# A graph-attention layer on one core: one-hots change engines, messages read their weights from PSUM, gathered rows enter as transposes

## The chip, the core and the metric

The kernel runs on one core of a Trainium2 chip. The core has TensorE (PE; PEld is its load of the stationary operand), VectorE (DVE), ScalarE (ACT), GpSimd (POOL) and SyncE (SP), which take their instructions in order and meet through semaphores. The two on-chip memories are SBUF and PSUM; PE writes its products into PSUM[...], and DVE and ACT can read and write PSUM too. The metric is device time in microseconds (us), the median of several runs.

## The reference, cut to what matters

A graph of 12500 nodes (128 features) and 200000 edges, sorted by destination, goes through two layers. The first is an attention layer with 4 heads of 32 channels:

```
xl, xr = x @ W_l, x @ W_r
e     = einsum(leaky_relu(xl[src] + xr[dst], 0.2), att)     # per edge and head
p     = exp(e - segment_max(e, dst)[dst])
out   = segment_sum(p / segment_sum(p, dst)[dst] * xl[src], dst) + bias + x
x1    = layernorm(x + layernorm(out) * gamma + beta)
```

with a self loop added for every node. The second layer takes `segment_sum(x1[src] + edge_attr, dst)`, a small two-matrix network and another layer norm.

## The kernel before

**Three stages.** A first stage (to about 60 us) computes xl for all nodes and stores it in DRAM as `xl_d`. The first layer (to about 2150 us) and the second (to the end) then go through the edges in 112 chunks of 1792: 128 partitions x T = 14 edges each. Because the edges are sorted, the destinations of a chunk span at most 128 consecutive nodes.

**The gathers.** For every chunk, `gather` (L186) issues 14 indirect DMAs on POOL, each of 128 rows of 512 bytes, into a tile `got` with four buffers. The first layer gathers from `xl_d`, the second from `x1_d`. The indices `srcs` lie in SBUF.

**One chunk of the first layer.** The functions below are called once per chunk c, several of them per quarter q (`quads`: three of 4 and one of 2 of the 14 columns).

- `nodes1/2/3` and `parts2/3` (L244 to L279) compute the destination side: xr of the chunk's nodes, split into three bf16 parts whose sum is the f32 value.
- `node_by_edge` (L281) builds a bf16 one-hot `odt`, nodes by edges, from the loaded destination numbers `row`, with one DVE compare per quarter (L285).
- `products` (L289) sums in PSUM tile `ph` (three buffers) xr[dst] and xl[src], transposed: three bf16 products of the parts with `odt` (L294), then for each column the gathered rows times an identity (L297).
- `leaky` (L300): ACT writes 0.2 times `ph` to `lk` (L304), DVE takes the larger of the two (L305).
- `away` (L309) and `edge_by_node0` (L315) build the other one-hot `od`, edges by nodes, in f32 on ACT: 14 times Abs(iota - rel), then one Relu(1 - od) over all columns (L312, L317).
- `scores` (L319): PE multiplies `lk` with the attention vector (L325).
- `weights1` to `weights5` (L332 to L385): running maxima of the scores over the edges of a node, by scans (L329) within a partition and across partitions, with transposes on PE between; then `val` gets the exponentials (L382).
- `messages` (L387): DVE multiplies the gathered rows with the exponentials, both in SBUF (L390).
- `sums` (L394): 14 products of `od` with `val` into `ps` (L398).
- `merge1`, `merge2`, `carry` (L402 to L433) bring in the self loop and a node that is cut by a chunk's end; `norm1a`, `roots`, `norm1b`, `norm2` (L458 to L487) do the layer norms of two chunks together and store x1.

**Order.** The loop at L499 writes out the order by hand: each engine's queue holds the instructions in the order of the calls. Iteration c works on chunk c (products to scores), on chunk c - 1 (weights to sums), on c - 2 (merge) and c - 3 (carry, norms), and prepares the destination side of c + 1. The gathers of c + 1 and, on SP, the loads of `row` and `x` for c + 2 are issued at its start. Tiles have two buffers unless noted.

The second layer's `edge_by_node` (L192) keeps its Abs and Relu on ACT.

Of the kernel before, what the change touches and what calls it, by code (L numbers as in the profile page):

```python
# [8 lines left out]
F32 = mybir.dt.float32  # L9
BF16 = mybir.dt.bfloat16  # L10
I32 = mybir.dt.int32
AF = mybir.ActivationFunctionType
OP = mybir.AluOpType
# [3 lines left out]
P = 128  # L17
D = 128
H = 4
C = D // H  # L20
HW = C + 1
AW = H * HW
RW = AW + H
VW = RW + 1
T = 14
CE = P * T
# [119 lines left out]
def fast_path(ctx: ExitStack, tc: tile.TileContext, a: dict, out: bass.AP, g: dict):  # L146
    nc = tc.nc
# [67 lines left out]
    with tc.tile_pool(name="ew", bufs=2) as ew, \  # L215
# [3 lines left out]
        keep = []  # L219
        for i in range(2):  # L220
            mask = ew.tile([P, H * S + 1], F32, name=f"mask{i}", bufs=1)
            nc.vector.memset(mask[:, H * S:], LOW)
            rf = ew.tile([H, P + 1], F32, name=f"rf{i}", bufs=1)
            nc.vector.memset(rf[:, 0:1], LOW)
            rb = ew.tile([H, P + 1], F32, name=f"rb{i}", bufs=1)
            nc.vector.memset(rb[:, P:], LOW)
            keep.append((mask, rf, rb))
        live = {}

        def put(name, c, tile_):  # L230
            live[name, c] = tile_
            return tile_
# [32 lines left out]

        def parts2(c):
            parts = live["parts", c]
            r1 = put("r1", c, ew.tile([P, D], F32, name="r1"))
            nc.vector.tensor_sub(r1, live.pop(("pn", c))[:, 3, :], parts[:, 0, :])
            nc.scalar.copy(parts[:, 1, :], r1)  # L270

        def parts3(c):
            parts = live["parts", c]
            nc.vector.tensor_sub(parts[:, 2, :], live.pop(("r1", c)), parts[:, 1, :])

        def nodes3(c):
            pm = ep.tile([P, 4 * P], F32, name="pm", bufs=2)
            nc.tensor.matmul(pm[:, :H], live.pop(("lks", c)), attm, start=True, stop=True)
            nc.vector.tensor_copy(live["sr", c][:, AW:RW], pm[:, :H])  # L279

        def node_by_edge(c, q):  # L281
            if q == 0:
                put("odt", c, ew.tile([P, CE], BF16, name="odt"))
            t0, m = quads[q]
            nc.vector.tensor_scalar(live["odt", c][:, t0 * P:(t0 + m) * P],  # L285
                                    live["row", c][:, t0 * P:(t0 + m) * P], nid[:, c:c + 1], None,
                                    op0=OP.is_equal)

        def products(c, q):  # L289
            t0, m = quads[q]  # L290
            ph = put("ph", (c, q), ep.tile([P, 4 * P], F32, name="ph", bufs=3))
            parts, odt, got = live["parts", c], live["odt", c], live["got", c]
            for k in range(3):
                nc.tensor.matmul(ph[:, :m * P], parts[:, k, :], odt[:, t0 * P:(t0 + m) * P],  # L294
                                 start=(k == 0), stop=False)
            for t in range(m):
                nc.tensor.matmul(ph[:, t * P:(t + 1) * P], got[:, t0 + t, :], ident,  # L297
                                 start=False, stop=(t == m - 1))

        def leaky(c, q):  # L300
            t0, m = quads[q]
# [2 lines left out]
            nc.scalar.mul(lk[:, :m * P], ph[:, :m * P], 0.2)  # L304
            nc.vector.tensor_max(lk[:, :m * P], ph[:, :m * P], lk[:, :m * P])  # L305


        def away(c, t0, t1):
            if t0 == 0:  # L309
                put("od", c, ew.tile([P, T, P], F32, name="od"))  # L310
            for t in range(t0, t1):
                nc.scalar.activation(live["od", c][:, t, :], iota[:, 0, :], AF.Abs,  # L312
                                     bias=nrel[:, c, t:t + 1])

        def edge_by_node0(c):  # L315
            od = live["od", c]
            nc.scalar.activation(od, od, AF.Relu, bias=1.0, scale=-1.0)  # L317

        def scores(c, q):  # L319
            t0, m = quads[q]  # L320
# [8 lines left out]
            nc.vector.tensor_tensor_scan(o, m, d, LOW, op0=OP.add, op1=OP.max)  # L329


        def weights1(c):  # L332
            mask, rf, rb = keep[c % 2]
            s = put("s", c, ew.tile([P, H * S], F32, name="s"))
            sv = s.rearrange("p (h s) -> p h s", h=H)
            nc.vector.memset(sv[:, :, 0:S:S - 1], LOW)
            nc.vector.tensor_scalar(mask[:, :H * S].rearrange("p (h s) -> p h s", h=H),
                                    same[:, c, None, :].to_broadcast([P, H, S]), -1.0, -LOW,
                                    op0=OP.add, op1=OP.mult)
            nc.scalar.copy(sv[:, :, 1:T + 1], live.pop(("sc", c)))  # L340
            fwd = put("fwd", c, ew.tile([P, H * S], F32, name="fwd"))
            bwd = put("bwd", c, ew.tile([P, H * S], F32, name="bwd"))
            scan(fwd, mask[:, :H * S], s)
            scan(bwd[:, ::-1], mask[:, :0:-1], s[:, ::-1])
# [24 lines left out]
        def weights5(c):  # L369
            mask, rf, rb = keep[c % 2]  # L370
            pm, s, fwd, bwd = (live.pop((k, c)) for k in ("pm", "s", "fwd", "bwd"))
            sv = s.rearrange("p (h s) -> p h s", h=H)
            nc.vector.tensor_copy(sv[:, :, 0:S:S - 1],
                                  pm[:, :2 * H].rearrange("p (k h) -> p h k", h=H))
            scan(fwd, mask[:, :H * S], s)
            scan(bwd[:, ::-1], mask[:, :0:-1], fwd[:, ::-1])
            mv = bwd.rearrange("p (h s) -> p h s", h=H)[:, :, 1:T + 1]
            arg = ew.tile([P, H, T], F32, name="arg")
            nc.vector.tensor_sub(arg, sv[:, :, 1:T + 1], mv)
            v = put("val", c, ew.tile([P, T, VW], F32, name="val"))  # L380
            vh = v[:, :, :AW].rearrange("p t (h c) -> p t h c", h=H)
            nc.scalar.activation(vh[:, :, :, C], arg.rearrange("p h t -> p t h"), AF.Exp)  # L382
            nc.scalar.copy(v[:, :, RW], lastf[:, c, :])
            nc.vector.tensor_mul(v[:, :, AW:RW], mv.rearrange("p h t -> p t h"),
                                 lastf[:, c, :, None].to_broadcast([P, T, H]))  # L385

        def messages(c, q):  # L387
            t0, m = quads[q]
            vh = live["val", c][:, t0:t0 + m, :AW].rearrange("p t (h c) -> p t h c", h=H)
            nc.vector.tensor_mul(vh[:, :, :, :C],  # L390
                                 live["got", c][:, t0:t0 + m, :].rearrange("p t (h c) -> p t h c", h=H),
                                 vh[:, :, :, C:].to_broadcast([P, m, H, C]))

        def sums(c):  # L394
            ps = put("ps", c, ep.tile([P, VW], F32, name="ps"))
# [98 lines left out]
        parts2(0)  # L494
        parts3(0)
        nodes3(0)
        for q in range(4):
            node_by_edge(0, q)
        for c in range(NCH + 2):  # L499
            on, nxt, prv, old = c < NCH, c + 1 < NCH, 0 < c <= NCH, c > 1  # L500
            k = (c - 3) // 2
            if c + 2 < NCH:
                load0(c + 2)
            if nxt:
                put("got", c + 1, gather(ew, xl_d, c + 1))
            if on:
                products(c, 0)
            if prv:
                weights1(c - 1)
            if on:  # L510
                away(c, 0, 3)
                leaky(c, 0)
            if prv:
                weights2(c - 1)
            if c > 2:
                carry(c - 3)
            if on:
                away(c, 3, 5)
                products(c, 1)
            if prv:  # L520
                weights3(c - 1)
            if on:
                leaky(c, 1)
                scores(c, 0)
            if old:
                merge1(c - 2)
            if prv:
                weights4(c - 1)
            if nxt:
                nodes1(c + 1)  # L530
            if prv:
                weights5(c - 1)
            if old:
                merge2(c - 2)
            if on:
                products(c, 2)
                leaky(c, 2)
                away(c, 5, 8)
                scores(c, 1)
            if nxt:  # L540
                nodes2(c + 1)
            if prv:
                messages(c - 1, 0)
            if nxt:
                parts2(c + 1)
            if prv:
                messages(c - 1, 1)
            if nxt:
                parts3(c + 1)
            if on:  # L550
                products(c, 3)
                leaky(c, 3)
                scores(c, 2)
            if prv:
                messages(c - 1, 2)
                messages(c - 1, 3)
            if nxt:
                nodes3(c + 1)
            if on:
                away(c, 8, T)  # L560
                scores(c, 3)
            if prv:
                sums(c - 1)
            if on:
                edge_by_node0(c)
            if nxt:
                for q in range(4):
                    node_by_edge(c + 1, q)
            if c % 2 == 1 and k >= 0:
                norm1a(k)  # L570
                roots(k)
            if c % 2 == 0 and k >= 0:
                norm1b(k)
                if k > 0:
                    norm2(k - 1)
# [558 lines left out]
```

## Time and profile before

| | |
|---|---|
| median of 3 runs | 4132.05 us (4130.75 to 4137.15) |
| the profiled execution | 4133.73 us, its span 4131.9 us |
| PE busy | 3270.6 us (79%) |
| PEld | 2777.0 us (67%) |
| DVE | 1741.6 us (42%) |
| ACT | 2047.6 us (50%) |
| POOL | 3060.0 us (74%) |
| gathers of the first layer | first 64.2 us, last 2112.7 us |
| gathers of the second layer | first 2150.1 us, last 4113.7 us |

A line of groups reads: source line, engine, operation, output <- inputs, partitions x elements and type, count | busy us in all, mean ns of one | idle time of the engine just before them, and what ended it. A line of the timeline reads: start us, duration us, engine, line, operation, operands, how many in a row, and in brackets the idle time before it and its releaser. "issue" is a wait for nothing that the profile shows. The granted clock is the share of TensorE's full clock that it was allowed.

### The profile page before, as it was taken

What the parts mean: (1) busy time and instruction counts of PE and PEld (TensorE: products, weight loads), DVE (VectorE), ACT (ScalarE), POOL (GpSimd) and SP (SyncE); (2) the same over time, 40 slices, a digit from 0 to 9 for tenths busy, and PEclk for the clock granted to TensorE, in tenths of its full rate; (3) what the DMA queues carried; (4) which work ended last, traced back from release to release, by engine and by line L of the source; (5) the groups of instructions that cost most, each with busy time, mean ns of one, the idle gap of its engine ahead of it and who ended that gap; (6) DMA issues with size and microseconds to landing.
All of it is one profiled execution on the core that took longest, in us unless ns stands there. A gap on an engine that the chain in (4) does not pass through costs nothing. (4 is left out here: it accounts for less than half of the span.)

```text
span 4131.9 us, 59032 instructions
## 1 busy us (share of the span) xinstructions
PE 3270.6 (79%) x19842; PEld 2777.0 (67%) x19842; DVE 1741.6 (42%) x6068; ACT 2047.6 (50%) x5502; POOL 3060.0 (74%) x3141
## 2 busy tenths in 40 slices
PE   5999898998999889989966776776766776766766
PEld 5887777787888778877755555555555555555555
DVE  3777777777777777777750101101010101010101
ACT  2666666666666666566653343434333333333332
POOL 2777777777777777777747777777777777777776
PEclk8989989889888998899887777777777777777776
DMA  6333333333333333333323333333333333333332
GB/s 204 106 107 112 110 105 112 102 112 113 109 107 104 109 112 112 102 113 103 111 72 109 100 120 100 121 100 119 101 111 109 111 109 112 109 103 116 94 118 70
DMA packets 236149, 451.41 MB, mean 109 GB/s; under 512 B 66104, under 2 KB 124601, under 8 KB 235836
## 3 DMA queue, kind: packets, MB, share of 16 engines
q0 software_dynamic: 100384, 205.04, 19.3%
q1 hardware_dynamic: 134876, 240.68, 17.3%
q8 instruction: 157, 2.57, 0.3%
q10 hardware_dynamic: 576, 1.84, 0.1%
q14 instruction: 156, 1.28, 0.1%
HBM read 426.22 MB, written 21.10 MB: 108 GB/s over the span
## 5 line engine op out<-in xcount | busy, mean ns | idle before, releaser
L186 POOL DMA_INDIRECT got<-xl_d,srcs x1568 | 1571.8, 1002 | 541.4 <-issue 505.4
L186 POOL DMA_INDIRECT got<-x_d,srcs x1568 | 1487.0, 948 | 514.0 <-issue 464.1
L613 PE MATMUL ps<-got,od 128*128 128x128 f32 x3136 | 850.6, 362 | 448.1 <-DMA got<-x_d,srcs 443.8
L613 PEld LDWEIGHTS ps<-got,od 128*128 128x128 f32 x3136 | 625.1, 248 | 591.1 <-DMA got<-x_d,srcs 588.6
L612 PE MATMUL ps<-ea,od 128*128 128x128 f32 x3136 | 773.4, 337 | 18.7 <-DMA ea<-in_edge_attr 18.7
L618 DVE SCALAR_TENSOR_TENSOR h<-x1w,ps 128x128 f32<-128x128 f32 x112 | 32.3, 288 | 1556.7 <-PE ps L613 1556.7
L612 PEld LDWEIGHTS ps<-ea,od 128*128 128x128 f32 x3136 | 631.8, 250 | 42.7 <-issue 42.7
L312 ACT ACTIVATE od<-iota,nrel 128x128 f32<-128x128 f32 x1568 | 503.6, 390 | 121.6 <-PE ps L398 121.5
L297 PEld LDWEIGHTS ph<-ident,got 128*128 128x128 f32 x3136 | 445.3, 201 | 164.7 <-DMA got<-xl_d,srcs 112.3
L297 PE MATMUL ph<-ident,got 128*128 128x128 f32 x3136 | 478.2, 290 | 91.1 <-DMA got<-xl_d,srcs 90.8
L398 PE MATMUL ps<-val,od 128*128 128x137 f32 x3136 | 498.7, 328 | 3.6 <-DVE val L390 3.6
L623 ACT COPY ns<-ps 128x128 f32<-128x128 f32 x111 | 29.4, 265 | 948.3 <-DVE h L618 948.3
L325 PE MATMUL sc<-attm,lk 128*128 128x4 f32 x3136 | 427.4, 257 | 71.8 <-DVE lk L305 71.3
L398 PEld LDWEIGHTS ps<-val,od 128*128 128x128 f32 x3136 | 479.8, 234 | 3.7 <-issue 3.7
L198 ACT ACTIVATE od<-iota,nrel 128x128 f32<-128x128 f32 x1568 | 479.9, 387 | 0.0
L325 PEld LDWEIGHTS sc<-attm,lk 128*128 128x128 f32 x3136 | 425.4, 209 | 80.8 <-DVE lk L305 79.5
L305 DVE TENSOR_TENSOR lk<-ph,lk 128x512 f32<-128x512 f32 x448 | 277.9, 620 | 314.4 <-ACT lk L304 314.3
L304 ACT ACTIVATE lk<-ph 128x512 f32<-128x512 f32 x448 | 241.7, 540 | 242.3 <-PE ph L297 242.0
L294 PE MATMUL ph<-odt,parts 128*128 128x512 bf16 (+1 forms) x1344 | 341.5, 365 | 1.3 <-DVE odt L285 1.3
L390 DVE TENSOR_TENSOR val<-got,val 128x512 f32<-128x512 f32 x448 | 267.3, 618 | 0.6 <-issue 0.4
L199 ACT ACTIVATE od<-od 128x896 f32<-128x896 f32 x224 | 212.7, 949 | 7.1
L294 PEld LDWEIGHTS <-parts 128*128 128x128 bf16 x1344 | 133.5, 106 | 96.9 <-issue 35.3
(139 smaller groups left out, 3213.4 us busy)
## 6 DMA issues: line engine op xcount, KB each, us to landing
ea<-in_edge_attr SPq DMA_DIRECT2D x111, 896.0 KB
row<-in_dst_rows SPq DMA_DIRECT2D x336, 256.0 KB
got<-xl_d,srcs POOLq DMA_INDIRECT x1568
got<-x_d,srcs POOLq DMA_INDIRECT x1568
row<-in_dst_rows SPq DMA_DIRECT2D x112, 128.0 KB
xg<-in_x_pad SPq DMA_DIRECT2D x112, 64.0 KB
x_d<-x1w SPq DMA_DIRECT2D x112, 64.0 KB
out<-y SPq DMA_DIRECT2D x111, 64.0 KB
```

The lines of the kernel that those rows point to most:

```text
L186: nc.gpsimd.indirect_dma_start(out=got[:n, t, :], out_offset=None, in_=table[:N, :], in_offset=bass.IndirectOffsetOnAxis(ap=srcs[:n, c, t: ...
L198: nc.scalar.activation(od[:, t, :], iota[:, 0, :], AF.Abs, bias=nrel[:, c, t:t + 1])
L294: nc.tensor.matmul(ph[:, :m * P], parts[:, k, :], odt[:, t0 * P:(t0 + m) * P], start=(k == 0), stop=False)
L297: nc.tensor.matmul(ph[:, t * P:(t + 1) * P], got[:, t0 + t, :], ident, start=False, stop=(t == m - 1))
L304: nc.scalar.mul(lk[:, :m * P], ph[:, :m * P], 0.2)
L305: nc.vector.tensor_max(lk[:, :m * P], ph[:, :m * P], lk[:, :m * P])
L312: nc.scalar.activation(live["od", c][:, t, :], iota[:, 0, :], AF.Abs, bias=nrel[:, c, t:t + 1])
L325: nc.tensor.matmul(live["sc", c][:, :, t0 + t], lk[:, t * P:(t + 1) * P], attm, start=True, stop=True)
L390: nc.vector.tensor_mul(vh[:, :, :, :C], live["got", c][:, t0:t0 + m, :].rearrange("p t (h c) -> p t h c", h=H), vh[:, :, :, C:].to_broadca ...
L398: nc.tensor.matmul(ps, od[:, t, :], v[:, t, :], start=(t == 0), stop=(t == T - 1))
L612: nc.tensor.matmul(ps, od[:, t, :], ea[:, t, :], start=(t == 0), stop=False)
L613: nc.tensor.matmul(ps, od[:, t, :], got[:, t, :], start=False, stop=(t == T - 1))
```

## The change

Only the first layer changes.

- A new PSUM tile `bank` takes one bank: it holds a copy of iota and, behind it, the exponentials of a chunk (`wts`). To make room, `ph` goes from three buffers to two.
- `node_by_edge` moves from DVE to ACT: Abs(row - nid), then Relu(1 - .) in place, over columns 0 to 1023 (half 0) and 1024 to 1791 (half 1).
- The other one-hot, `od`, moves from ACT to DVE: one compare per quarter of iota (from `bank`) with `rel`. It is built one iteration later than before, and has one buffer.
- `weights1` is split: `weights0` prepares its inputs; both now end the iteration of the chunk's own products. `weights5` is split too: `weights6` lets ACT write the exponentials to `wts` and copy them to `val`.
- `messages` reads the exponentials from `wts` in PSUM instead of from `val`.
- `products` first puts the gathered rows into `ph` as PE transposes and then adds the three bf16 products.
- `parts2` keeps its difference in the PSUM tile `pn` instead of an SBUF tile.
- The order of the calls in the loop is new.

```diff
+        bank = ep.tile([P, P + T * H], F32, name="bank")
+        nc.vector.tensor_copy(bank[:, :P], iota[:, 0, :])
+        wts = bank[:, P:].rearrange("p (t h) -> p t h", h=H)
+        nnid = ew.tile([P, NCH], F32, name="nnid", bufs=1)
+        nc.vector.tensor_scalar(nnid, nid, -1.0, None, op0=OP.mult)
...
-        def node_by_edge(c, q):
...
-            nc.vector.tensor_scalar(live["odt", c][:, t0 * P:(t0 + m) * P],
-                                    live["row", c][:, t0 * P:(t0 + m) * P], nid[:, c:c + 1], None,
-                                    op0=OP.is_equal)
+        def node_by_edge(c, i, step):
...
+            lo, hi = (0, 8 * P) if i == 0 else (8 * P, CE)
+            o = live["odt", c][:, lo:hi]
+            if step == 0:
+                nc.scalar.activation(o, live["row", c][:, lo:hi], AF.Abs, bias=nnid[:, c:c + 1])
+            else:
+                nc.scalar.activation(o, o, AF.Relu, bias=1.0, scale=-1.0)
 
         def products(c, q):
...
-            ph = put("ph", (c, q), ep.tile([P, 4 * P], F32, name="ph", bufs=3))
+            ph = put("ph", (c, q), ep.tile([P, 4 * P], F32, name="ph", bufs=2))
             parts, odt, got = live["parts", c], live["odt", c], live["got", c]
+            for t in range(m):
+                nc.tensor.matmul(ph[:, t * P:(t + 1) * P], got[:, t0 + t, :], ident,
+                                 start=(t == 0), stop=False, is_transpose=True)
             for k in range(3):
                 nc.tensor.matmul(ph[:, :m * P], parts[:, k, :], odt[:, t0 * P:(t0 + m) * P],
-                                 start=(k == 0), stop=False)
-            for t in range(m):
-                nc.tensor.matmul(ph[:, t * P:(t + 1) * P], got[:, t0 + t, :], ident,
-                                 start=False, stop=(t == m - 1))
+                                 start=False, stop=(k == 2))
...
-        def away(c, t0, t1):
...
-        def edge_by_node0(c):
-            od = live["od", c]
-            nc.scalar.activation(od, od, AF.Relu, bias=1.0, scale=-1.0)
+        def edge_by_node0(c, q):
+            t0, m = quads[q]
+            if q == 0:
+                put("od", c, ew.tile([P, T, P], F32, name="od", bufs=1))
+            nc.vector.tensor_tensor(live["od", c][:, t0:t0 + m, :],
+                                    bank[:, None, :P].to_broadcast([P, m, P]),
+                                    rel[:, c, t0:t0 + m, None].to_broadcast([P, m, P]), op=OP.is_equal)
...
+        def weights6(c):
+            v = live["val", c]
             vh = v[:, :, :AW].rearrange("p t (h c) -> p t h c", h=H)
-            nc.scalar.activation(vh[:, :, :, C], arg.rearrange("p h t -> p t h"), AF.Exp)
+            nc.scalar.activation(wts, live.pop(("arg", c)).rearrange("p h t -> p t h"), AF.Exp)
+            nc.scalar.copy(vh[:, :, :, C], wts)
             nc.scalar.copy(v[:, :, RW], lastf[:, c, :])
...
         def messages(c, q):
...
-                                 vh[:, :, :, C:].to_broadcast([P, m, H, C]))
+                                 wts[:, t0:t0 + m, :, None].to_broadcast([P, m, H, C]))
```

The calls of an iteration in their new order, with on, nxt, prv, old standing for chunks c, c + 1, c - 1, c - 2 (loads and gathers first, as before; carry of c - 3):

```
prv weights2   prv edge_by_node0(0)   carry   on products(0)
prv weights3   prv edge_by_node0(1)   on leaky(0)   on products(1)   nxt node_by_edge(0, Abs)
prv edge_by_node0(2)   prv weights4   on leaky(1)   prv edge_by_node0(3)   on scores(0)
on products(2)   on leaky(2)   old merge1   nxt nodes1   on scores(1)   on products(3)
prv weights5   on leaky(3)   prv weights6   old merge2   nxt node_by_edge(0, Relu)   on scores(2)
prv messages(0)   nxt nodes2   prv messages(1)   nxt parts2   prv messages(2)   nxt parts3   prv messages(3)
on scores(3)   nxt nodes3   on weights0   on weights1   prv sums
nxt node_by_edge(1, Abs)   nxt node_by_edge(1, Relu)   norms as before
```

## The prediction

> **What bounds the kernel now.** I first read the page's busy shares. PE leads with 79%, but these are means over two layers, so I went to the stretches: in 1000 to 2000 us (first layer) PE is busy 902 us at a granted clock of 0.90, DVE 734, ACT 625, POOL 767; in 3000 to 4000 (second layer) PE is busy 697 and POOL 757. The page's chain of work that ended last covers only the last microsecond and says nothing. The costliest groups say what POOL does, first layer, then second:
>
> ```profile
> L186 POOL DMA_INDIRECT got<-xl_d,srcs x1568 | 1571.8, 1002 | 541.4 <-issue 505.4
> L186 POOL DMA_INDIRECT got<-x_d,srcs x1568 | 1487.0, 948 | 514.0 <-issue 464.1
> ```
>
> The same 1568 gathers last 1002 ns in the first layer and 948 in the second. Between two there is a gap of 0.30 us. 14 gathers x (1.002 + 0.304) = 18.28 us; a chunk takes 18.3 us by the spacing of its repeating rows. So POOL never stops, and its sum is the layer's time: 112 x 18.3 = 2050 us. The waits of 500 to 1500 us (us in all, times, longest) agree:
>
> ```profile
> POOL got L186 <- issue: 211.8, 695, 0.3
> DVE lk L305 <- ACT lk L304: 148.3, 117, 3.6
> PE ph L297 <- DMA got<-xl_d,srcs: 47.5, 44, 2.3
> ```
>
> POOL's waits are the bare gap, whatever name they carry; PE on its part catches up with the gathers and waits for them about 0.9 us a chunk. POOL leads, the others follow.
>
> Next: why 1002 and not 944, the median of both layers? The timeline of POOL, and that of DVE, over one chunk (start us, duration us):
>
> ```profile
> 1037.02 1.44 POOL L186 DMA_INDIRECT got<-xl_d,srcs  x1 [0.30 <-issue]
> 1038.77 1.33 POOL L186 DMA_INDIRECT got<-xl_d,srcs  x1 [0.30 <-issue]
> 1040.40 1.05 POOL L186 DMA_INDIRECT got<-xl_d,srcs  x1 [0.30 <-issue]
> 1041.76 0.94 POOL L186 DMA_INDIRECT got<-xl_d,srcs  x1 [0.30 <-issue]
> ```
>
> ```profile
> 1036.96 0.68 DVE L390 TENSOR_TENSOR val<-got,val 128x512 f32<-128x512 f32 x1
> 1038.10 1.02 DVE L390 TENSOR_TENSOR val<-got,val 128x512 f32<-128x512 f32 x2
> 1039.10 1.53 DVE L285 TENSOR_SCALAR odt<-row,nid 128x512 bf16<-128x512 int32 x4
> 1041.41 0.42 DVE L479 TENSOR_TENSOR x1w<-x1w,L_gnn_ln_gamma 128x256 f32<-128x256 f32 x1
> 1044.49 0.66 DVE L305 TENSOR_TENSOR lk<-ph,lk 128x512 f32<-128x512 f32 x1
> ```
>
> Three of 14 gathers are long: each starts while L390 or L285 runs and is late by about what is left of it (1037.64 - 1037.02 = 0.6 us against 0.5 lost). I laid all POOL rows of 150 to 2050 us over the DVE rows. The 1453 gathers exceed 0.944 us by 83.3 us in all. 168 that overlap an L285 carry 48.1 us of it, 225 more that overlap only an L390 30.0, the rest 5.2. Of 374 that overlap L305 (one input in PSUM) and neither of the two, 5 are over 0.99 us, mean 0.943; 353 beside scans: mean 0.942. Scaled to the layer: 1568 x (1.002 - 0.944) = 91 us lost.
>
> **The change, part by part.**
>
> *L285 goes to ACT, L390 reads its weights from PSUM.* Both long kinds with all inputs in SBUF vanish; L390 becomes L305's kind. A gather then falls to 0.944 + 5.2/1453 + 0.001 = about 0.949, which is also what the second layer shows (0.948). POOL's sum loses 1568 x (1.002 - 0.949) = **83 us**. [...] Such instructions stay: scans 1.17 us a chunk, the small merges 2.2, norms 1.7, about 5.1 us beside 4.3 removed (L390 2.47, L285 1.82). By time held, 4.3/9.4 of 91 us would go: 42 us, 4090. The rows say that the short ones cost 5.2 of 83. I take the row, since a short instruction leaves little to wait for, and keep 42 as an end.
>
> *New one-hots on DVE* (three of 512, one of 256 columns, iota in PSUM): not in the trace; nearest is L305, 0.687 and 0.418 us, so +2.48 us a chunk. L285 (3 x 0.492 + 0.346 = 1.82) goes: DVE +0.66. From below they could go at L285's pace (+0), from above at twice L305's (+3.1). DVE is busy 13.4 us a chunk, and some 45 instructions have 0.03 us between dependent neighbours: 13.4 + 0.7 + 1.3 = 15.4 us dense. [...] L305 from PSUM (687 ns) and L390 from SBUF (684) show none. I add none.
>
> *ACT.* Off: 14 Abs at 1.85/6 = 0.31 and the 1792-wide Relu, 1.70: -6.0. On: Abs and Relu over 1024 and 768 columns; from 1792 in 1.697 and 896 in 0.949 follow 1.06 and 0.84, 3.8 in all, and a small copy 0.2. ACT 11.4 -> 9.4 us a chunk. An int32 input isn't in the trace; at double price ACT has 13.2, still under the gathers.
>
> *Transposes in place of identity products.* L297: 8 records (4 products) in 1.05 us, 0.26 each. The first stage's transposes (L129) take 0.93 us for 7, 0.13 each: PE loses 14 x 0.13 = 1.8 us a chunk, 16.5 -> 14.7. If they cost as much as products, PE stays at 16.5, under 17.5.
>
> All this is hidden: the gathers take 14 x (0.949 + 0.304) = **17.54 us** a chunk, and DVE 15.4, PE 14.7, ACT 9.4 lie beside them. If that cover goes, each 0.1 us a chunk costs 11 us.
>
> *Order and buffers.* No DMA is added or moved; the row loads on SP now wait for ACT's one-hot instead of DVE's, a chunk before use. The gathers on POOL wait only for messages three chunks back. The new ring to watch is ph with two buffers: leaky(0) on DVE, then scores(0) and products(2) on PE, the 0.2 multiple on ACT, then leaky(2) on DVE, with merge1, weights5 and the messages queued behind it. Scores 0.95 (8 records of L325), products 0.5 + 0.65, ACT 0.6, handovers 0.3: 3.0 us, of which one-hots and leaky(1) fill about 2. Bubble 1.0. In every second chunk the root's table loads (1.28 us each) hold the copy of rm: 0.4 on the mean. Followers: 15.4 + 1.0 + 0.4 = 16.8, under 17.54 by 0.7. od with one buffer: the first one-hot waits for the sums of a chunk before, matmul by matmul; from there through the messages to the next sums is about 13.6 us, no bound.
>
> Start and drain: 37 us pass between the layers' gathers (2112.7 to 2150.1). The one-hots add 2.2 us there, scans ahead of the roots save about 1.3: +1, within -3 to +4.
>
> **Sum.** Span 4131.9 and 1.8 around it are 4133.7 for the profiled execution; the median of runs is 1.7 lower. 4133.7 - 83 + 1 - 1.7 = **4050 us**.
>
> **Rivals.**
>
> *A. POOL stays the bound, at clean pace* (above): 4050; with the ends of residue (all 91 us gone, or 25 left) and drain 4038 to 4072. Chance 0.62.
>
> *B. The followers take over part.* The 0.7 us margin is an estimate from rows of another order. At 17.9 us a chunk, 0.4 x 112 = 45 of 91 saved, about 4092; span 4072 to 4123. For it: DVE's waits on ACT's multiple, 2.7 us a chunk now. Against: most of these come where PE waits for gathers. Chance 0.17.
>
> *C. Only the one-hots' share goes* [...]: 48.1/83.3 x 91 = 53 saved, 4080. Against: L305 writes as much. Or nothing goes, because late gathers have another cause: no change, 4132; the overlap counts speak against that. Chances 0.08 and 0.03.
>
> *D. Slower: PE's clock.* [...] The row: the stage before the layers (0 to 60 us), where one PE record in three is a transpose, was granted 0.94, the first layer 0.90, and the second, without transposes in its stream, 0.74. If PE ran at half clock throughout, eight score records take 1.7 us (as they do at 1015.7) and the ring is 5 us long, bubble 3: 15.4 + 3.0 + 0.4 = 18.8 us a chunk, + 0.5 x 112 = 56, 4188. It decides from a bubble of 2.5 on, three quarters of the time at half clock. By today's clock a fifth of it is. Chance 0.10.
>
> **How the numbers follow.** The forecast is A's. The range 4038 to 4095 holds A, C and half of B, about 0.8. Faster by over 0.2% (8 us, about what a measurement of this kernel can tell): A, B and C, 0.87; same 0.03; slower 0.10.
>
> **What would show it.** Right: gathers of got<-xl_d near 0.95 us, none over 1.2 beside the messages; POOL's idle still 0.30 us each; PE's and DVE's waits on got growing or steady. Wrong: POOL waiting for messages by more than the gap (B, D), mean gathers at 0.97 and above (C), clock under 0.7 in the first layer (D).

## The result, and the profile after

The median of six runs after is 4069.28 us (4065.99 to 4072.12), before 4133.47 (six runs): the ratio is 0.9843, with a 95% interval of 0.983 to 0.9856. The change saves 64 us where 82 were forecast; 4069 lies inside the range of 4038 to 4095, 19 us above the 4050 named. The profiled execution took 4072.12 us, its span 4070.3.

The costliest groups of the changed kernel, gathers of the first and second layer (busy us, mean ns, then the idle time before them):

```profile
L186 POOL DMA_INDIRECT got<-xl_d,srcs x1568 | 1501.9, 958 | 540.9 <-issue 488.4 <-PE ph L302 11.9 <-DVE xb L468 4.9
L186 POOL DMA_INDIRECT got<-x_d,srcs x1568 | 1488.5, 949 | 521.1 <-issue 468.0 <-ACT od L198 43.7 <-DMA got<-x_d,srcs 7.9
```

The mean gather of the first layer fell from 1002 to 958 ns, not to the 949 of the prediction. The waits of 500 to 1500 us (total, times, longest) and the busy sums of 1000 to 2000 us (PE, PEld, DVE, ACT, POOL, granted clock, DMA share, GB/s):

```profile
POOL got L186 <- issue: 215.1, 706, 0.3
ACT lk L312 <- PE ph L305: 173.4, 123, 3.9
DVE lk L313 <- ACT lk L312: 106.9, 163, 3.5
```

```profile
1000.00:2000.00 1000.00, 897.64 (x5567) 753.17 (x5622) 800.47 (x2699) 536.22 (x1194) 758.63 (x793) 0.85 0.39 112
```

POOL's waits are still the bare gap of 0.3 us, none longer. So the gathers still set the layer's pace: 14 x (0.958 + 0.304) = 17.67 us against a measured spacing of 17.68 from chunk to chunk (18.30 before). The followers do wait for one another (ACT for the products up to 3.9 us), yet POOL never waits for them. 44 ns on each of 1568 gathers is 70 us, more than the 64 that were saved.

The other term is the drain. POOL stood idle for 43.7 us between the last gather of the first layer (start 2042.2) and the first of the second (2086.9); before it was 36.5: +7 us. -70 + 7 = -63, and the second layer ends 1.6 us later; the span is down by 61.6.

Which gathers are still late? POOL's and DVE's timelines after, over the end of one chunk (start us, duration us):

```profile
1081.13 0.95 POOL L186 DMA_INDIRECT got<-xl_d,srcs  x1 [0.30 <-issue]
1082.38 0.94 POOL L186 DMA_INDIRECT got<-xl_d,srcs  x1 [0.30 <-DVE val L403]
1083.63 1.57 POOL L186 DMA_INDIRECT got<-xl_d,srcs  x1 [0.30 <-issue]
1085.50 0.94 POOL L186 DMA_INDIRECT got<-xl_d,srcs  x1 [0.31 <-issue]
```

```profile
1081.17 0.68 DVE L403 TENSOR_TENSOR val<-got,bank 128x512 f32<-128x512 f32 x1
...
1083.63 0.41 DVE L468 TENSOR_TENSOR xb<-xg,L_gnn_ln_beta 128x256 f32<-128x256 f32 x1
1083.96 0.42 DVE L492 TENSOR_TENSOR x1w<-x1w,L_gnn_ln_gamma 128x256 f32<-128x256 f32 x1
1084.41 0.42 DVE L493 TENSOR_TENSOR x1w<-x1w,xb 128x256 f32<-128x256 f32 x1
```

The gather at 1081.13 begins beside a message (L403) and takes 0.95. The one at 1083.63 begins with the norm's sum of x and beta (L468, two inputs in SBUF), stays behind it and the multiplication by gamma (L492), and takes 1.57.

I sorted all 1568 gathers of each trace by the DVE operation that was in progress 0.1 to 0.2 us after the gather began (a gather can stand in two rows; late is over 0.99 us; the excess is over 0.944):

| DVE operation beside the start | inputs | before: gathers, mean us, late, excess us | after |
|---|---|---|---|
| messages, L390 / L403 | before SBUF + SBUF, after SBUF + PSUM | 236, 1.172, 149, 53.8 | 249, 0.947, 6, 0.8 |
| compare of int32, L285 | SBUF | 118, 1.194, 113, 29.5 | gone |
| one-hots `od`, L319 | PSUM + SBUF | none | 271, 0.944, 0, 0.1 |
| larger of two, L305 / L313 | PSUM + SBUF | 257, 0.946, 8, 0.6 | 226, 0.944, 0, 0.0 |
| norms' sum of x and bias or beta, L455 / L468 | SBUF + SBUF | 38, 1.116, 26, 6.6 | 27, 1.326, 23, 10.3 |
| norms' gamma and additions | SBUF + SBUF | 55, 1.041, 34, 5.3 | 71, 1.074, 51, 9.2 |

All excess was 91.6 us before and is 21.7 after. The first row is the cleanest of it: the same instruction in the same shapes, with only its second input moved from SBUF to PSUM, and the lateness is gone. A new order could also have moved the gathers away from the messages, but it did not: before, of 152 gathers that began inside a message with at least 0.19 us of it left, 146 were late, and the 152 lost 0.35 us each in the mean; after, 169 began so and none was late. One of these, with its message:

```profile
1184.67 0.95 POOL L186 DMA_INDIRECT got<-xl_d,srcs  x1 [0.30 <-issue]
```

```profile
1184.37 0.68 DVE L403 TENSOR_TENSOR val<-got,bank 128x512 f32<-128x512 f32 x1
```

### The profile page after: what moved, and what is told of

It is laid out like the page before. It is cut to its first block, busy times and chain, and to the rows that moved or that the text cites. A ratio compares the mean times of both kernels' runs of the same rounds, so it can differ in the third digit from the quotient of the medians.

```text
span 4070.3 us, 55444 instructions
## 1 busy us (share of the span) xinstructions
PE 3228.6 (79%) x18162; PEld 2678.9 (66%) x18274; DVE 1820.0 (45%) x6070; ACT 1825.0 (45%) x4382; POOL 2991.6 (73%) x3141
## 3 DMA queue, kind: packets, MB, share of 16 engines
q1 hardware_dynamic: 134876, 240.68, 17.6%
## 5 line engine op out<-in xcount | busy, mean ns | idle before, releaser
L186 POOL DMA_INDIRECT got<-xl_d,srcs x1568 | 1501.9, 958 | 540.9 <-issue 488.4
L633 PEld LDWEIGHTS ps<-ea,od 128*128 128x128 f32 x3136 | 640.4, 253 | 44.3 <-issue 25.7
L411 PE MATMUL ps<-val,od 128*128 128x137 f32 x3136 | 586.7, 367 | 6.1 <-DVE val L403 6.1
L411 PEld LDWEIGHTS ps<-val,od 128*128 128x128 f32 x3136 | 568.9, 271 | 6.2 <-issue 5.2
L198 ACT ACTIVATE od<-iota,nrel 128x128 f32<-128x128 f32 x1568 | 479.9, 387 | 0.0
L644 ACT COPY ns<-ps 128x128 f32<-128x128 f32 x111 | 29.5, 266 | 950.8 <-DVE h L639 950.8
L313 DVE TENSOR_TENSOR lk<-ph,lk 128x512 f32<-128x512 f32 x448 | 278.3, 621 | 231.1 <-ACT lk L312 229.4
L305 PE MATMUL ph<-odt,parts 128*128 128x512 bf16 (+1 forms) x1232 | 320.2, 366 | 7.9 <-ACT odt L295 1.7
L302 PE MATMUL ph<-ident,got 128*128 128x128 f32 x1568 | 279.1, 290 | 48.0 <-DMA got<-xl_d,srcs 47.3
L319 DVE TENSOR_TENSOR od<-bank,rel 128x512 f32<-128x512 f32 x448 | 272.1, 608 | 60.7 <-PE ps L411 60.6
L403 DVE TENSOR_TENSOR val<-got,bank 128x512 f32<-128x512 f32 x448 | 274.0, 613 | 0.9 <-issue 0.5
L302 PEld LDWEIGHTS ph<-ident,got 128*128 128x128 f32 x1568 | 198.8, 155 | 108.9 <-DMA got<-xl_d,srcs 54.3
L293 ACT ACTIVATE odt<-row,nnid 128x1024 bf16<-128x1024 int32 x224 | 233.6, 1043 | 0.0
```

What stands on the lines that cost most here:

```text
L186: nc.gpsimd.indirect_dma_start(out=got[:n, t, :], out_offset=None, in_=table[:N, :], in_offset=bass.IndirectOffsetOnAxis(ap=srcs[:n, c, t: ...
L198: nc.scalar.activation(od[:, t, :], iota[:, 0, :], AF.Abs, bias=nrel[:, c, t:t + 1])
L319: nc.vector.tensor_tensor(live["od", c][:, t0:t0 + m, :], bank[:, None, :P].to_broadcast([P, m, P]), rel[:, c, t0:t0 + m, None].to_broadca ...
L403: nc.vector.tensor_mul(vh[:, :, :, :C], live["got", c][:, t0:t0 + m, :].rearrange("p t (h c) -> p t h c", h=H), wts[:, t0:t0 + m, :, None] ...
L411: nc.tensor.matmul(ps, od[:, t, :], v[:, t, :], start=(t == 0), stop=(t == T - 1))
L633: nc.tensor.matmul(ps, od[:, t, :], ea[:, t, :], start=(t == 0), stop=False)
```

## The experiments

On the chips where the experiments ran, the kernel before took 5559 to 5659 us in place of 4133. In the trace of e5_before_msgs, within 0.2% of it, POOL waited in 1000 to 1500 us for TensorE's scores (147.0 us in 15 waits, the longest 12.0) and ACT for signals that the view calls `remote` (110.9 us in 18 waits, the longest 8.9). So I read a time there as what an edit costs when TensorE's chain sets the pace, and only the durations of single gathers speak on the gathers. Where that shows in a trace is told under the last experiment.

### Which kinds of DVE operation hold a gather (e4_kinds)

The changed kernel, with seven more DVE operations in each chunk of the second layer; the kind changes every 16 chunks. The first layer is untouched.

```diff
+            for i in range(7):
+                if kind == 1:
+                    nc.vector.tensor_mul(so, sa, sb)
+                if kind == 2:
+                    nc.vector.tensor_mul(so, sa, sp)
+                if kind == 3:
+                    nc.vector.tensor_scalar(sh, si, nid[:, c:c + 1], None, op0=OP.is_equal)
+                if kind == 4:
+                    nc.vector.tensor_scalar(so, sp, 2.0, None, op0=OP.mult)
+                if kind == 5:
+                    nc.vector.tensor_mul(so[:, :256], sa[:, :256], sb[:, :256])
+                if kind == 6:
+                    nc.vector.tensor_mul(so[:, :128], sa[:, :128], sb[:, :128])
```

`sp` lies in PSUM, the others in SBUF; `si` is int32, `sh` bf16.

> The changed kernel; its second layer, where VectorE is nearly idle, gets seven extra VectorE instructions per chunk, whose results nobody reads, of one kind for 16 chunks each: none; two SBUF inputs x 512 (f32); SBUF and PSUM x 512; compare of int32 from SBUF to bf16 x 512; f32 from PSUM times 2 x 512; two SBUF inputs x 256; two SBUF inputs x 128. Theory: gathers of the stretches with two SBUF inputs and with the int32 compare rise (by 0.02 to 0.10 us each at 512), those with a PSUM input stay at 945 to 950 ns; 256 rises less than half as much as 512, 128 hardly. By time held alone (each kind with two SBUF inputs holds for its length): 128 would cost a fifth to a fourth of 512, 256 half. Rival (any long VectorE instruction holds): all kinds of 512 rise alike.

Measured: 5815.51 us in one run. POOL's timeline in a chunk of kind 1, and DVE's there:

```profile
4102.46 0.95 POOL L186 DMA_INDIRECT got<-x_d,srcs  x1 [0.30 <-issue]
4103.72 1.15 POOL L186 DMA_INDIRECT got<-x_d,srcs  x1 [0.30 <-issue]
4105.17 1.15 POOL L186 DMA_INDIRECT got<-x_d,srcs  x1 [0.30 <-issue]
4106.63 1.15 POOL L186 DMA_INDIRECT got<-x_d,srcs  x1 [0.30 <-issue]
4108.08 0.94 POOL L186 DMA_INDIRECT got<-x_d,srcs  x1 [0.30 <-issue]
```

```profile
4102.66 5.03 DVE L698 TENSOR_TENSOR so<-sa,sb 128x512 f32<-128x512 f32 x7
```

The three gathers inside the run of L698 are 0.21 us late, the next one is on time. Over all gathers that overlap each kind:

| kind | gathers | mean us | over 0.99 |
|---|---|---|---|
| SBUF + SBUF, 512 columns | 64 | 1.140 | 51 |
| SBUF + SBUF, 256 | 49 | 1.044 | 27 |
| SBUF + SBUF, 128 | 37 | 0.950 | 3 |
| SBUF + PSUM, 512 | 78 | 0.943 | 0 |
| PSUM alone, 512 | 79 | 0.943 | 0 |
| compare of int32 in SBUF, 512 | 64 | 0.943 | 0 |

Beside operations with two inputs in SBUF the gathers took 1.140, 1.044 and 0.950 us at 512, 256 and 128 columns; with one of the two in PSUM 0.943, and none was late. That is what the prediction took for the messages, shown away from the change. Where a gather began 0.09 us or more inside an operation that had at least 0.19 us left, it was late by what was left less 0.13 us: 49 of 49 gathers in the first row, 16 of 16 in the second, none of 31 and none of 32 in the two rows with PSUM. The compare held no gather, but no gather of its stretch began so deep in a compare, so this row does not clear the compares. The compares themselves show a delay. Durations of one instruction (least, median, most ns) by line:

```profile
L698 DVE TENSOR_TENSOR so<-sa,sb x112: 671/692/694, 3823.5 to 4136.2; 128x512 f32<-128x512 f32 x112
L700 DVE TENSOR_TENSOR so<-sa,sp x112: 667/686/690, 4164.2 to 4469.0; 128x512 f32<-128x512 f32 x112
L702 DVE TENSOR_SCALAR sh<-si,nid x112: 468/487/696, 4497.1 to 4799.2; 128x512 bf16<-128x512 int32 x112
```

36 of the 112 compares took 0.55 to 0.70 us in place of 0.487; the other two kinds show no such spread. So here it was compares that ran up to 0.2 us longer, with the gathers on time (0.943). In this run every gather beside a compare began less than 0.03 us after the compare's start, or ahead of it; what a compare that is well under way does to a gather is seen in e2_odt_dve below.

### One part undone at a time, in the changed kernel (e1, e2, e3)

```diff
-                                 wts[:, t0:t0 + m, :, None].to_broadcast([P, m, H, C]))
+                                 vh[:, :, :, C:].to_broadcast([P, m, H, C]))
```

> The changed kernel, but the messages read their weights from SBUF again, as before (the copy in val). Theory (a message with two SBUF inputs holds a gather that starts beside it): the first layer's gathers go from 958 ns to about 990 (before, the gathers beside messages alone carried 30 us of excess and more where the compares followed), time 4069 + 40 to 55, about 4115. Rival (only the removed compare on VectorE mattered, a message holds by its write): 958 ns and 4069 +- 4.

> The changed kernel (4069 us, first-layer gathers 958 ns), its messages reading the weights from val in SBUF again, nothing else. If two SBUF inputs hold the gathers: where POOL sets the pace (the kernel before at about 4133 us), the messages' own share of the lateness comes back, 30 to 55 us: 4100 to 4125, gathers at 977 to 993 ns, the late ones beside the 512-wide products. If only the compares held them: 4069 +- 8, gathers at 958. Where TensorE sets the pace instead (the kernel before above 5500 us), both theories give a time within 1% of the changed kernel, and only the gathers beside the products speak.

e1_msgs_sbuf: 5786.64 us, 1.0236 [1.021, 1.0262] of before; e1b_msgs 5796.55, 1.0254 [1.0226, 1.0282]. Gathers 953 and 951 ns: no share came back. This is a miss and no evidence: not one of the 1568 gathers of either run began beside a message, since POOL stood idle at that place of the chunk (1869 us of idle time before the gathers of the first layer in e1_msgs_sbuf, 541 in the changed kernel on record above). The spacing of the first layer is 29.58 us, and 29.61 in e4_kinds, whose first layer is the changed one: where TensorE's chain leads, the memory of the weights made no difference.

```diff
-            o = live["odt", c][:, lo:hi]
-            if step == 0:
-                nc.scalar.activation(o, live["row", c][:, lo:hi], AF.Abs, bias=nnid[:, c:c + 1])
-            else:
-                nc.scalar.activation(o, o, AF.Relu, bias=1.0, scale=-1.0)
+            t0, m = quads[2 * i + step]
+            nc.vector.tensor_scalar(live["odt", c][:, t0 * P:(t0 + m) * P],
+                                    live["row", c][:, t0 * P:(t0 + m) * P], nid[:, c:c + 1], None,
+                                    op0=OP.is_equal)
```

> The changed kernel, but the bf16 one-hot is made by VectorE compares again, two at each of the places where ScalarE now has its Abs and Relu. Theory: each compare of int32 from SBUF holds a gather that starts beside it; in ones and twos, rather than four in a row, they cost less than the 48 us of before: gathers at 970 to 985 ns, time 4090 to 4110. If VectorE's 1.5 us more a chunk makes it the bound, POOL waits for messages and the time is over 4110. Rival (the compares never held anything): 958 ns, 4069.

> The changed kernel with the bf16 one-hot made by four compares on DVE again, in place of Abs and Relu on ACT, nothing else. If a compare (int32 in, bf16 out) holds a gather that begins inside it, and the gathers set the pace (the kernel before at about 4133 us): 4085 to 4110, gathers at 968 to 985 ns. If the compares were late companions of the messages and hold nothing of their own: 4069 +- 8, gathers at 958 to 962. Where TensorE sets the pace (the kernel before above 5500 us): the gathers beside the compares alone decide, 0.944 or above 1.0.

e2_odt_dve: 5691.7 us, 1.0074 [1.0051, 1.0097]; e2b_compares 5701.57, 1.0083 [1.0057, 1.011]. 172 and 168 gathers began beside a compare; 50 and 44 of them were late, with an excess of 7.0 and 5.9 us. Two gathers of e2_odt_dve with the DVE rows beside them, the first late, the second not:

```profile
1000.35 1.17 POOL L186 DMA_INDIRECT got<-xl_d,srcs  x1 [0.30 <-issue]
...
1022.82 0.95 POOL L186 DMA_INDIRECT got<-xl_d,srcs  x1 [11.29 <-issue]
```

```profile
1000.23 0.47 DVE L291 TENSOR_SCALAR odt<-row,nid 128x512 bf16<-128x512 int32 x1
1000.62 0.67 DVE L317 TENSOR_TENSOR od<-bank,rel 128x512 f32<-128x512 f32 x1
...
1022.76 0.78 DVE L291 TENSOR_SCALAR odt<-row,nid 128x512 bf16<-128x512 int32 x2
```

The first begins 0.12 us into a compare, which has 0.35 us left, and loses 0.23. The second begins 0.06 us into a pair and loses nothing; the compare beside it takes 0.515 us in place of 0.478. So gathers are late beside compares alone, with no message near, and which of the two takes longer goes with where in the compare the gather begins. A gather that began 0.09 us or more into a compare with at least 0.19 us left was late in every case on record: 112 of 112 in the kernel before, 41 of 41 in e2_odt_dve, 40 of 40 in e2b_compares, 14 of 14 in e11_after_blocks, 2 of 2 in e5_before_msgs, and in the two e2 runs the loss was what was left less 0.13 us. A gather that began less than 0.09 us into a compare, or ahead of it, was on time in 357 of 364 cases of these runs and e4_kinds.

The third part undone: `is_transpose=True` taken out of L302, which makes the transposes identity products again.

> The changed kernel with identity products in place of the transposes, in the same places. Theory: PE has 1.8 us a chunk more and stays hidden behind the gathers: 4069 +- 6, gathers 958 ns; the first layer's granted clock goes back up from 0.84 to about 0.90, if transposes are what lowered it. Rival (PE was near the bound, the transposes were needed): over 4085, and POOL waits for messages.

5920.12 us, 1.0473 [1.0445, 1.0501]. The groups of these products on PE, in e3_identity and then in e1_msgs_sbuf, which keeps the transposes:

```profile
L302 PE MATMUL ph<-ident,got 128*128 128x128 f32 x3136 | 569.7, 332 | 2.3 <-issue 1.5
```

```profile
L302 PE MATMUL ph<-ident,got 128*128 128x128 f32 x1568 | 327.9, 337 | 0.0
```

A transpose is one record (337 ns), an identity product two of about the same length (332 ns). The first layer's spacing is 30.59 us against 29.61 with transposes (e4_kinds): they save 1.0 us a chunk here, and nothing of rival D's loss shows. The granted clock of 1000 to 2000 us is 0.68 without transposes and 0.62 with them, so in this pair they do come with a lower clock.

### One part alone, in the kernel before (e5, e6, e7)

e5_before_msgs writes the exponentials to a PSUM bank as well and lets the messages read them there, with `ph` at two buffers (first diff); e6_before_odt makes the bf16 one-hot by Abs and Relu on ACT in the old order of calls (second diff); e7_before_both has both.

```diff
+            nc.scalar.activation(wts, arg.rearrange("p h t -> p t h"), AF.Exp)
+            nc.scalar.copy(vh[:, :, :, C], wts)
...
-                                 vh[:, :, :, C:].to_broadcast([P, m, H, C]))
+                                 wts[:, t0:t0 + m, :, None].to_broadcast([P, m, H, C]))
```

```diff
-            t0, m = quads[q]
-            nc.vector.tensor_scalar(live["odt", c][:, t0 * P:(t0 + m) * P],
...
+            i, step = q // 2, q % 2
+            lo, hi = (0, 8 * P) if i == 0 else (8 * P, CE)
+            o = live["odt", c][:, lo:hi]
+            if step == 0:
+                nc.scalar.activation(o, live["row", c][:, lo:hi], AF.Abs, bias=nnid[:, c:c + 1])
+            else:
+                nc.scalar.activation(o, o, AF.Relu, bias=1.0, scale=-1.0)
```

> The kernel before with one part of the change alone: the exponentials go to PSUM and the messages read them there (ph has two buffers to make room). Theory: the messages' share of the 91 us goes, gathers fall from 1002 to 965 to 975 ns, time 4132 - 40 to 55, about 4085, unless ph with two buffers slows PE in the old order. Rival (messages hold by their write): 1002 ns, 4132.

> The kernel before with the other part alone: the bf16 one-hot by Abs and Relu on ScalarE, at the old place at the end of an iteration. Theory: the compares' share goes, gathers at 975 to 985 ns, 30 to 45 us less, about 4095, if ScalarE with 3.8 us a chunk more (15.2 of 18.3) keeps pace. Rival (ScalarE becomes the bound, which is why the other one-hot had to leave it): POOL waits for messages, time 4110 to 4200.

> The kernel before with both parts, but the old order, the f32 one-hot on ScalarE and identity products: ScalarE 15.4 us and PE 16.5 us a chunk beside gathers of 17.6. Theory: if the followers keep pace, gathers near 955 ns and 4065 to 4075, the drain of before kept (a few us better than the change). Rival: ScalarE's queue makes the chunk longer than the gathers' 17.6, POOL waits, 4080 to 4150.

Measured: 5567.3 us, 1.0018 [1.0008, 1.0028]; 5740.93, 1.0325 [1.0303, 1.0346]; 5726.55, 1.0302 [1.0282, 1.0321]; gathers 971, 958 and 960 ns. In e5_before_msgs 108 gathers began beside a compare and three were late: 106 of them began when less than 0.19 us of it was left. Its late ones stand beside the norms (51 beside L458, the sum with beta, mean 1.546, 30.7 us of its 42 us of excess). So the mean gathers of these three tell of the norms, not of the parts that were tried. What the times show is another thing: with TensorE's chain in the lead, the one-hot made by two ACT passes costs 1.5 us a chunk in the old order (spacing 29.29 in e7_before_both, 27.82 in e5_before_msgs, which differs from it only in keeping the compares) and 0.9 in the new one (29.61 in e4_kinds, 28.70 in e2_odt_dve). ACT's 0.2 multiple stands behind these passes in its queue, which may be why; that wasn't tried by itself.

### The norms' inputs moved (e8_norms)

The changed kernel with gamma and beta in the PSUM bank, so that two of the three 256-wide operations of the second norm have one input in SBUF:

```diff
-            o, xb, n = both(k, "L0_gnn_ln_beta")
-            nc.vector.tensor_mul(o, o, rows["L0_gnn_ln_gamma"].to_broadcast([P, n, D]))
-            nc.vector.tensor_add(o, o, xb)
+            nc.vector.tensor_mul(o, o, gam.to_broadcast([P, n, D]))
+            nc.vector.tensor_add(o, o, bet.to_broadcast([P, n, D]))
+            nc.vector.tensor_add(o, o, live["x", c0][:, :n])
```

> The changed kernel; gamma and beta of the norm in the first layer lie in PSUM beside the weights, so that two of the three 256-wide instructions there have one SBUF input. Theory: of the 19 us by which the gathers of the changed kernel still exceed 944 ns, 12 or so lie beside these; gathers go from 958 to 949 to 952 ns, time 4069 - 8 to 14, about 4058. Rival (the residue is not from two SBUF inputs): 4069.

5653.26 us, 1.0174 [1.0155, 1.0193]; gathers 951 ns, excess 10.8 us. 51 gathers began beside an operation that now reads the bank, the addition of beta: mean 0.943 us, none late, though 0.2 us of it was left. Another 51 began beside the sum with the bias, which still has two inputs in SBUF: mean 1.160, all late, 11.0 us (the other gathers are a little below 0.944). Both are 256 wide and stand in the same norms, so this pair points to the two inputs in SBUF for most of the residue: 16.4 of its 21.7 us stand beside the norms' 256-wide operations. What the version is worth where the gathers lead could not be seen here; the residue that it can reach is a part of the 21.7 us.

### PE's work cut, four blocks of chunks in one kernel (e11, e12)

To bring the gathers back into the lead, both kernels leave out the three bf16 products and 13 of the 14 sums of each chunk of the first layer. In blocks of 28 chunks the messages' second input and the engine of the bf16 one-hot are switched:

```diff
+            wt = vh[:, :, :, C:] if (c // 28) % 2 else wts[:, t0:t0 + m, :, None]
...
+            if c // 56:
+                t0, m = quads[2 * i + step]
+                nc.vector.tensor_scalar(live["odt", c][:, t0 * P:(t0 + m) * P],
+                                        live["row", c][:, t0 * P:(t0 + m) * P],
+                                        nid[:, c:c + 1], None, op0=OP.is_equal)
+                return
```

> The changed kernel with PE's work cut so that the gathers set the pace: the three bf16 products and 13 of the 14 sums of a chunk of the first layer are left out (the output is not the reference's, and the whole time says nothing). Four blocks of 28 chunks: 0 as the changed kernel; 1 messages read val in SBUF; 2 the bf16 one-hot by four compares on DVE; 3 both. Read per block: mean gather and chunk spacing (14 gathers and 14 gaps of 0.30). If each of the two holds gathers on its own: block 0 at 0.945 to 0.96 us, block 1 at 0.97 to 0.99, block 2 at 0.97 to 0.99, block 3 at 0.99 to 1.02; spacing 17.5, 17.8, 17.8, 18.2. If only two SBUF inputs hold: blocks 0 and 2 alike, 1 and 3 alike and later by 0.03 or more. If only the compares hold: 0 and 1 alike, 2 and 3 alike.

> The kernel before with the same cut of PE's work and the same four blocks in the old order of calls: 0 messages from PSUM and one-hot on ACT; 1 messages from SBUF; 2 one-hot by compares on DVE; 3 both, as the kernel before. Where the gathers set the pace: block 3 near the recorded 1.00 us and 18.3 us a chunk. If each holds alone, by the shares of the prediction (48 for the compares, 30 for the messages, of 83): block 0 at 0.95, block 1 at 0.97, block 2 at 0.98, block 3 at 1.00. If only two SBUF inputs hold: 0 and 2 alike, 1 and 3 alike. If only the compares hold: 0 and 1 alike, 2 and 3 alike.

| block | e11: mean gather us, spacing us | e12 |
|---|---|---|
| 0 neither | 0.953, 24.6 | 0.958, 26.6 |
| 1 messages from SBUF | 0.954, 24.9 | 0.960, 26.7 |
| 2 compares on DVE | 0.966, 25.7 | 0.973, 25.8 |
| 3 both | 0.968, 26.7 | 0.973, 26.5 |

The cut did not do what it was for: the spacing stayed far over the gathers' 17.6 us. By the means alone only compares hold gathers; the starts forbid that reading. In e11 one gather began beside a message in block 1 and three in block 3, and all four were late (1.37, and 1.24 in the mean). Beside compares began 45 in block 2, with 1.2 us of its excess of 8.8; most of the rest moved with the norms, which now met their gathers 0.15 us more deeply (11 gathers beside the sum with bias or beta, 1.146 us in block 0; 13, 1.301 in block 2). In e12 26 gathers began beside compares in block 2 and none was late: each began with less than 0.19 us of the compare left. So the +0.014 us of block 2 over block 0 is mostly a shift of phase between norms and gathers.

These traces show what the slow pace is like. PE's and ACT's timelines in e11_after_blocks, block 1, rows between left out:

```profile
1013.16 0.67 PE L308 MATMUL ph<-ident,got 128*128 128x128 f32 x2
...
1016.18 1.06 PE L259 MATMUL pn<-wlr,xT 128*128 128x256 f32 x2
1024.04 0.80 PE L332 MATMUL sc<-attm,lk 128*128 128x4 f32 x3 [6.80 <-DVE lk L316]
```

```profile
1014.01 0.25 ACT L253 COPY xT<-pn 128x128 f32<-128x128 f32 x1
1023.14 0.39 ACT L315 ACTIVATE lk<-ph 128x256 f32<-128x256 f32 x1 [8.89 <-remote]
```

The two transposes that L315 reads are down as ended at 1013.83, and ACT goes on at 1023.14, with nothing else before it. Either their ends, which the profile models, are wrong by some 9 us, or the signal was late; no row tells which, and it comes back about once a chunk. That is probably also why leaving out PE's work did not help.

## Why the prediction was right, point by point

**POOL sets the layer, and the followers hide.** Right. POOL's waits are 706 x 0.3 us and no longer one. DVE's busy time is 800/1000 x 17.68 = 14.2 us a chunk (13.4 + 0.7 = 14.1 was counted), ACT's 9.5 (9.4). PE's is 15.9, not 14.7: the granted clock went from 0.90 to 0.85 and a record of the sums takes 367 ns, before 328. 17.68 - 15.9 leaves 1.8 us a chunk of cover, where 2.8 was counted.

**Gathers to 949 ns, -83 us.** The mechanism was right, for messages and compares; the size was not: 958 ns, -70. The term that was mis-sized is the residue: 949 ns leave 1568 x 0.005 = 8 us of excess, and 21.7 were measured. Two things were missed. The smaller one is the booking: every gather that overlapped an L285 was put on L285, also where a norm's 256-wide operation with two SBUF inputs came right behind the compares and held it on (in the trace before, 13 gathers began across L285 and the sum with the bias, mean 1.360; 12 of them owe 4.0 us to the sum). With these 4.0, the excess before that was neither the messages' nor the compares' was 12.5 us, not 8. The larger one is that the residue was carried over as it stood, while the new order shifts the gathers against the norms: beside the norms' 256-wide operations, some 10.5 us of excess became 16.4. By the operation in progress as the gather begins, messages carried 54 us and compares 29 (25 without the sums' share), where the prediction had 30 and 48. Since both went, their sum nearly held, and that is luck: its split would have misled anyone who made only one half of the change.

**The estimate by time held.** If each DVE operation with two inputs in SBUF cost the gathers in proportion to its own length, an estimate of mine from the 4.3 of 9.4 us a chunk that go, as much as 49 of 91 us would have stayed. The measured residue, 21.7, lies between that and my 8. That short operations leave little to wait for holds at 128 columns (0.950 in e4_kinds) and no longer at 256 (1.044), and the norms are 256 wide.

**One-hots on DVE.** 0.67 and 0.41 us, predicted 0.687 and 0.418. I had added nothing for a source in PSUM, and none was needed: the messages' median is 679 ns with it, 682 before without. **Abs from int32:** 1.14 us for 1024 columns and 0.95 for 768 (1.06 and 0.84 estimated).

**Drain +1.** Wrong: +7, outside its own bounds of -3 to +4. DVE's timeline after, behind the last gather's start at 2042.23:

```profile
2057.89 0.69 DVE L319 TENSOR_TENSOR od<-bank,rel 128x512 f32<-128x512 f32 x1 [1.37 <-PE ps L411]
...
2059.50 1.58 DVE L319 TENSOR_TENSOR od<-bank,rel 128x512 f32<-128x512 f32 x3
...
2064.13 2.21 DVE L403 TENSOR_TENSOR val<-got,bank 128x512 f32<-128x512 f32 x4
```

The last products come 5.0 us after the last gather's start (2.6 before), as the followers run later behind POOL. The messages start 16.9 us after these products (13.2 before): the sums of the chunk before end 2.2 us later, and the one-hots, which wait for these sums to free `od`'s only buffer and then stand ahead of the last chunk's weights, add 1.5. From there to the next gathers it is 22.7 us (21.7). 2.4 + 3.7 + 1.0 = 7.1, nearly all of the 7.2. I had counted only the one-hots' own 2.2 us, less some scans.

The 13 us that the gathers fell short and the 6 of the drain make the 19 by which 4050 was missed.

**Rivals.** B and D did not come: POOL never waited. That transposes lower the clock, on which D rests, was not shown by the rows of before (0.94, 0.90, 0.74). The clock did sink, from 0.90 to 0.85; its price stayed under the cover, and e3_identity shows the transposes as a gain where PE's chain leads. C, a message that holds gathers by what it writes, whatever its second input, is refuted by the changed kernel itself: 249 gathers beside messages, 0.947 us. Two ends were summed loosely: B's own terms give 4132 - 45 + 1 = 4088, not 4092, and A's slow end is 4133.7 - 66 + 4 - 1.7 = 4070, not 4072. The measured 4069 stands close to that end.

What stays open: in no experiment did the gathers set the pace, so the shares of messages and compares are read from the trace before, not from the time of a kernel with one half of the change. Two buffers for `od` with earlier one-hots for the last chunk, which should give back some of the drain, were not tried.

## What to carry to other kernels

Where gathers issued on POOL set the pace, look in the trace at what DVE is doing as each gather begins. Here a 512-wide operation with both inputs in SBUF, under way with at least 0.19 us left, made the gather late by what was left less 0.13 us (49 of 49 in e4_kinds); with one input in PSUM the gathers took 0.943 us (0.947 beside the changed messages), and DVE no longer (679 ns a message, 682 before). Book a late gather on the operation in progress at its start, and on one behind it only where it ends the wait, not on any that it overlaps, or the saving of one edit is put on another. An edit that moves the order also moves which operations the gathers meet (10.5 us beside the norms became 16.4 here). And when an engine off the path is filled up, cost the drain by the order in its queue, not by the time it adds (+7 us here, +1 predicted).

## What was not expected of the hardware

Of a gather and an int32-to-bf16 compare side by side, either can be the longer one: a gather of e2_odt_dve that began 0.12 us into a compare was 0.23 us late, and in e4_kinds, where each began less than 0.03 us into one or ahead of it, compares took up to 0.2 us longer with the gathers on time (0.943). And on other chips the same kernel before took 5559 to 5659 us; the trace of e11_after_blocks there has ACT go on some 9 us after the records of the products that it reads end. The changed kernel was not run there by itself; e1b_msgs, whose first layer has its spacing, took 1.0254 of before, so a change that pays where the gathers lead can cost where TensorE's chain does.
